# A four-layer graph stack on one core: row loads reordered, plane copies tied behind roundings, maps of h put ahead at a change of pair

## The chip, the cores and the metric

The kernel runs on one core of a Trainium2 chip. The metric is the device time of one execution in microseconds (us); the time of a version is the median of its runs. The engines have short names here: PE is the matrix engine (PEld its weight loads), DVE the vector engine, ACT the scalar engine, POOL the GpSimd engine and SP the sync engine, which here only issues DMAs. Each engine works through its own queue of instructions in order.

## The reference, cut to what matters

`x` is 8 batches of 2048 nodes with 64 features; `adj` is a 2048 x 2048 row-normalised adjacency matrix in float32. Four layers follow each other, each of them `x = x + layer(relu(layernorm(x)), adj)`:

```
layer 0:  A1 = A;  A2 = 2 A A - I;  out[n] = sum_k (A_k h)[n] @ w[n,k] + b[n]
          with w[n,k] = sum_d emb[n,d] W[d,k],  b[n] = emb[n] @ bias   (d = 16, k = 3)
layer 1:  v = h with node 0 set to a given vector; three times:
          v = relu([v, A v] @ W1.T + b1) @ W2.T + b2
layer 2:  (A h) * c, mixed by two small weights, then @ w_out.T + b_out
layer 3:  attention with mask adj > 0.5, softmax, then elu
```

The kernel uses that every row of `adj` has one value for all its non-zero entries and that no entry exceeds 0.5. It tests both on the way. If a test fails, a flag sends the program into a second, general path; with these inputs the flag stays 0. With no entry above 0.5 the mask of layer 3 is empty, its softmax is uniform, and its attention is the mean of h over all nodes.

## The kernel before, in words

**Tiling.** The 8 batches are four pairs p; a pair's two batches of 64 features fill 128 partitions. The 2048 nodes are 16 chunks m of 128 and four blocks nb of 512. `BT` holds the sign pattern (0 or 1) of the whole matrix in SBUF, 16 rows of chunks of 1 MiB. A product with the matrix is 16 chunks times two matmuls of 128 x 512: an operand is split into a rounded part H (`halves`, L274: an ACT copy to the fast matmul type) and the rest L (L282: a DVE subtraction that reads H), and both are multiplied with `BT` (L305). The factor of each row (`crow`) is applied when PSUM is read (`scaled`, L287, its DVE instruction L290).

**Loading (L380 to L660).** POOL issues the loads of the 16 rows (`load_adj`, L387), of the blocks of `x` (L155), of the four blocks on the diagonal `dg` (`load_dg`, L374; these give each row's value) and of the weights. `pool_loads` (L395) chains them in the order of a list. `plan[k]` is the list of what is issued after the k-th POOL power instruction (`powers`, L239, the 1/sqrt of the layer norm). ACT turns each row into signs in two halves (`sign`, L412). PE runs 8 matmuls of pair 0 and 6 of pair 1 as soon as a row is signed (`step`, L553). `bias_products` (L470) are two float32 matmuls with DVE copies to `bnb`. `make_cols` (L381) takes the diagonal on DVE, `make_crow` (L419) turns it by PE (`pt_c`) and DVE.

**Layer 0 (`node_weights`, L811).** For each of 4 blocks x 4 sub-blocks t, PE computes `y` (L825) in two groups of 12 matmuls from the three operands t0T, t1T, t2T, and DVE adds it into `acc` and `odd` with the embeddings (L834, 8 instructions each). `y` has two buffers in PSUM. After each t the function `between(nb, t)` (L877) runs side work: `join_planes` (t0T of the next block, ACT L195), `split_next`, which pops one `store_planes` (L172, two ACT copies into the single buffer `pl`, then a POOL DMA to DRAM, L173), and `halve_next`, which makes H and L of the next pair's operand (for pair 0 from PE transposes `pt_t`).

**Layers 1 and 2.** `step1` (L1013) is one of the three steps of layer 1 for a pair: sums of A v (`chunks`), maps by weights (`map_two`, `ph`, L1024), an addition and relu (`add`, L1057, L1058), and the maps of the result (`finish_two`, `back_two` L750, 64 small matmuls to `bn`). `finish_two` of blocks 2 and 3 is put off by `carry` into the next step or the next pair. At a change of pair, `halve_two` (again `back_two`, to `bn_u`) makes the new pair's last two operands from `gT`; it stands ahead of the carried `finish_two`. `layer2` works the same way with one product for each block. `go_on` (L253) advances the layer norms that are under way by a stage; `ahead` names a DVE instruction that they are put behind. At the end, `sums`, `keep_warm` (matmuls that nobody reads, L112) and `outputs` (L1194, L1199) finish layer 3.

**What sets the order.** The program is written as one sequence; a list scheduler with its own model of times turns it into the engines' queues, and may put a later instruction ahead of an earlier one on the same engine when it takes the earlier for not ready. `with tc.issue_after(ins):` adds an edge: the block's instructions on the engine of `ins` stand behind `ins` in that queue. It adds no semaphore.

```
plan = {
    1: ((row, 5), (xb, 4), (row, 6)), 2: ((xb, 5), (row, 7), (load_emb, 0)),
    3: ((row, 8),), 4: ((load_bias, 0), (row, 9), (xb, 6)),
    5: ((row, 10), (xb, 7), (row, 11), (row, 12)), 6: ((row, 13), (dia, 0), (row, 14)),
    7: ((row, 15), (dia, 1), (dia, 2), (dia, 3)) + tuple((load_wt, i) for i in range(K)),
}
```

Of the kernel before, what the change touches and what calls it, by code (L numbers as in the profile page):

```python
# [32 lines left out]
def kernel(tc: tile.TileContext, *args):  # L33
    nc = tc.nc
    with tc.tile_pool(name="flagp", bufs=1) as flagp:
        flag = flagp.tile([1, 1], I32, name="flag")
        uniform_path(tc, flag, *args)
        other = nc.values_load(flag[0:1, 0:1], min_val=0, max_val=1)
        with tc.If(other > 0):
            general_path(tc, *args)  # L40

# [2 lines left out]
def uniform_path(  # L44
# [132 lines left out]
    def split_next():  # L177
        if splits:
            splits.pop(0)()
# [381 lines left out]
    for _ in range(2):  # L561
        load_x01(nc.sync)
    row, dia, xb = load_adj, load_dg, lambda k: load_x01(nc.gpsimd)
    pool_loads(order[0], (
        (row, 0), (row, 1), (xb, 2), (row, 2), (xb, 3), (row, 3), (row, 4),
    ))
    with tc.issue_after(order[-1].ins):
        order.append(make_mask())
    for i in range(2):
# [12 lines left out]
    stage(1, 2)  # L582
    plan = {
        1: ((row, 5), (xb, 4), (row, 6)), 2: ((xb, 5), (row, 7), (load_emb, 0)),
        3: ((row, 8),), 4: ((load_bias, 0), (row, 9), (xb, 6)),
        5: ((row, 10), (xb, 7), (row, 11), (row, 12)), 6: ((row, 13), (dia, 0), (row, 14)),
        7: ((row, 15), (dia, 1), (dia, 2), (dia, 3)) + tuple((load_wt, i) for i in range(K)),
    }
    with tc.issue_after(order[-1].ins):
        pool_loads(powers[1], plan[1])  # L590
    for m in range(NCH):
        if m == 12:
            sign(14)
            sign(15)
            low()
            behind_v(lambda: turn_emb(last))
        if m % 2 and m < 12:
            k = m // 2 + 2
            norm_block(k)
            pool_loads(powers[k], plan[k])  # L600
            if k == 6:
                with tc.issue_after(order[-1].ins):
                    order.append(nc.gpsimd.tensor_tensor(
                        bd.rearrange("p (j c) -> p j c", c=C), bias8.to_broadcast([P, 8, C]),
                        mask.to_broadcast([P, 8, C]), op=ALU.mult,
                    ))
        if m == 13:
            behind_v(lambda: bias_products(last))

            def columns():  # L610
                for q in range(NB):
                    make_cols(q)
            behind_v(columns)
        last = step(0, m, banks[0])
        if m > 0:
            with tc.issue_after(last.ins):
                last = step(1, m - 1, banks[1])
        if m > 13:
            with tc.issue_after(last.ins):
                for nb in (0, 1) if m == 14 else (2, 3):  # L620
                    make_crow(nb)
# [112 lines left out]
        return lastp[0].tile([P, 512], F32, tag="fm", name=name, bufs=4)  # L734

    two = (slice(0, C), slice(C, P))

    def back_two(fTs, wmat, name):

        ps = psums[-1].tile([P, 2, 512], F32, tag="big", name=f"bn_{name}")
        for i, fT in enumerate(fTs):
            for t in range(4):
                for hf in range(2):
                    for bb in range(2):
                        at = t * P + hf * C
                        nc.tensor.matmul(  # L750
                            ps[two[hf], bb, (4 * i + t) * C:(4 * i + t + 1) * C],
                            fT[two[bb], at:at + C], wmat[two[bb], two[bb]],
                            start=True, stop=True,
                        )
        return ps.rearrange("p b (t c) -> p t b c", c=C)

    def back_whole(fT, wmat, name):
# [97 lines left out]
    for p in range(NP):  # L855
        hl_next, t1T_next = [], []

        loaded = {}

        def load_next(q):  # L860

            nm = f"0_{p + 1}_{q}"
            if p == 0:
                loaded[q] = l0q.tile([P, 512], F32, tag="hb", name=f"t1b_{nm}", bufs=3)
                nc.scalar.dma_start(loaded[q], t1D[:, q * 512:(q + 1) * 512])
            elif p + 1 < NP:
                loaded[q] = load_h(p + 1, q, nm, l0q)

        def halve_next(q):
            if q in loaded:  # L870
                src = loaded.pop(q)
                with tc.issue_after(chain[-1].ins):
                    hl_next.append(
                        back(src, 1, q) if p == 0 else halves(src, f"0_{p + 1}_{q}")
                    )

        def between(nb, t):  # L877

            if t == 2 and ahead_t0:
                join_planes(*ahead_t0)  # L880
            split_next()
            if t == 0 and 4 * p + nb + 1 < 4 * NP:
                at = divmod(4 * p + nb + 1, NB)
                ahead_t0.extend((load_planes(0, *at, l0q), term(0, "t0T_%d_%d" % at)))
            if t == 1 and p == 0:
                restage()
            if p + 1 == NP and t == 3 and nb > 1:
                begin_next(0, 3 * (nb - 2))
            if 4 * p + nb + 1 == 4 * NP:
                if t == 0:  # L890
                    begin_next(0, 2)
                if t < 3:
                    first_operand(t)
            elif nb == 2 and t == 1:
                halve_next(0)
            elif nb == 3:
                halve_next(t + 1)
                if t == 0:
                    load_next(3)

        def reload_t1(q):
            t = term(1, f"t1T_0_1_{q}")
            nc.sync.dma_start(t, t1D[:, q * 512:(q + 1) * 512])
            t1T_next.append(t)

        if p > 1:
            steps = make_weights()

            def behind(nb):
                if p + 1 < NP:  # L910
                    norm_0(p + 1, nb)
                elif nb in (0, 2):
                    next(steps)

            t1T, hl1 = term1(p, hl, behind)
        for nb in range(NB):
            nm = f"0_{p}_{nb}b"
            crow = load_crow(nb, nm)
            t2T = product(
                hl1, nb, nm, term(2, f"t2T_{nm}"), crow,  # L920
                fill={5: lambda: first_t0.append(
                    to_feat(h_first, term(0, "t0T_0_0"), "0_0_0")
                )} if p + nb == 0 else {},
                tag="mm" if p + nb else "b6",
            )
            if p + nb == 0:
                t0T = first_t0[0]
            go_on()
            ahead_t0 = []
            if p + nb == 0:  # L930
                pro.close()
                psums.append(ctx.enter_context(
                    tc.tile_pool(name="psum", bufs=2, space=bass.MemoryType.PSUM)
                ))
            if p == 0:
                restage()
            if nb == 3:
                load_next(2)
            if 4 * p + nb + 1 == 4 * NP:
                begin_next(0, 1)  # L940
            node_weights(p, nb, (t0T, t1T[nb], t2T), between)
            t0T = ahead_t0[-1] if ahead_t0 else None
            if nb in (1, 2):
                load_next(nb - 1)
            with tc.issue_after(kept[-1].ins):
                m = 4 * p + nb
                nc.gpsimd.dma_start(rows_of(MD, m), BTf[:, m, :])
            if p == 0:
                reload_t1(nb)
                norm_0(2, nb)  # L950
        if p == 0:
            hl1, t1T = hl_next, t1T_next
        else:
            hl = hl_next
# [58 lines left out]
    def step1(n, p, st, hl, gT):  # L1013
# [15 lines left out]
                for bb in range(2):  # L1029
                    nc.scalar.copy(gT[nb + i][two[bb], :], ph[bb][two[bb ^ i], :])  # L1030

        def finish_two(nb):
            ps = back_two(g_new[nb:nb + 2], w2T if last else w1e2, f"{nm}_{nb}")
            if not last:
                nc.vector.tensor_tensor(ps, ps, rows4(r1e, 8), op=ALU.add)
            for i in range(2):
# [32 lines left out]
        if st == 0:  # L1069
            fill = {4: lambda: begin_next(n, 3)} if n else {7: lambda: first_operand(3)}  # L1070
        chunks(ps0, hl, 0, halves_of[0], fill)
        if other:
            halve_two(n, 2)
        if carry:
            carry.pop()()
        map_two(0)
        ps1 = sums_of(1)
        chunks(ps1, hl, 1, halves_of[0])
# [12 lines left out]
        chunks(ps2, hl, 2, range(NCH), fill)  # L1091
        scale(ps2, 2)
        map_two(2)
        finish_two(0)
        add(2)
        go_on()
        fill = {}
# [9 lines left out]
        scale(ps3, 3)  # L1107
        add(3)
        go_on()
        carry.append(lambda: finish_two(2))  # L1110
        return hl_new, g_new

    def layer1(n, p):
# [19 lines left out]
    def finish2(g, count=1):  # L1133

        pn = back_two(es[g:g + count], wos, f"2_{g}")
        for i in range(count):
# [8 lines left out]
                acc, nm, lambda h: zs.update({k: h})  # L1145
            )
            later.append(norm) if i else norm()

    def sums(g):

# [13 lines left out]
        if nb == NB - 1 or g + 2 == NP * NB:  # L1164
            if not final:
# [11 lines left out]
                totals.append(total)  # L1177
                if g + 2 == NP * NB:
                    totals.pop()()
                    keep_warm("mm", 20)  # L1180
            else:
                for t in range(4):
                    nc.tensor.matmul(
# [4 lines left out]
    def outputs(p):  # L1188

        for nb in range(NB):  # L1190
# [5 lines left out]
                    op0=ALU.mult, op1=ALU.add  # L1196
                )
            queue = nc.scalar if nb % 2 == 0 and p == NP - 1 else nc.sync
            queue.dma_start(runs_of(out, p, nb), runs(acc))  # L1199

    def layer2(n, p):
        hl, _ = ops[n]
# [5 lines left out]

        def maps(g):
            if g == 0:  # L1210
                return carry.pop()()
            for k in (g - 4, g - 3):
                if k >= 0:
                    sums(k)
# [35 lines left out]
    for n, (layer, p) in enumerate(items):  # L1250
        (layer1, layer2)[layer - 1](n, p)
        if n == NP - 1:
            test_end()


@with_exitstack
# [590 lines left out]
```

## Time and profile before

| what | value |
|---|---|
| median of 3 runs | 1186.31 us (1185.85 to 1187.0) |
| the profiled execution's own time | 1184.05 us |
| its span, first to last instruction | 1182.3 us |
| PE busy | 1156.7 us, 98% of the span |
| DVE, ACT, POOL busy | 743.6, 293.6, 244.8 us |
| granted PE clock, mean | 0.995 |
| DMA | 147.02 MB, mean 124 GB/s |
| the chain that ended last | PE 78%, DVE 7%, DMA 5%, issue 4%, POOL 3%, ACT 2% |

The page has one column for each engine; busy is the union of its instructions. A wait stands in square brackets: how long the engine had been idle, and the instruction that ended it. In the timeline a row is start, duration, engine, line, operation, output and inputs. In the table by stretches each engine has its busy time and number of instructions, and PEclk is the share of the full clock that PE was granted. An idle PE is what this kernel can lose; on the other engines idle time costs nothing by itself.

### The profile page before, as it was taken

Reading aid. Unit: us, or ns where it says so; the run is one execution under the profiler, and the core shown is the slowest. Engines: PE = TensorE matmul, PEld = TensorE weight load, DVE = VectorE, ACT = ScalarE, POOL = GpSimd, SP = SyncE. Lnnn points to the kernel's source line nnn. Section 1 sums busy time; section 2 is a strip of 40 time slices with the busy share of each in tenths; the row PEclk is TensorE's granted clock in tenths of the full one; section 3 lists DMA queues with packets and bytes.
Section 4 is the critical chain, followed back from the end, with each engine's and each line's share of the span. In section 5 each row is a group of like instructions: output and inputs, shape, how many; then the busy total and the mean of one; then the engine's idle time right before and its main releaser. Section 6 shows DMA issues by size and latency. Waiting matters only on the chain.

```text
span 1182.3 us, 19454 instructions
## 1 busy us (share of the span) xinstructions
PE 1156.7 (98%) x7614; PEld 803.1 (68%) x7614; DVE 743.6 (63%) x1933; ACT 293.6 (25%) x465; POOL 244.8 (21%) x259
## 2 busy tenths in 40 slices
PE   9999999999999999999999999999999999999995
PEld 7775545555585555855557777777777777788884
DVE  5457878877847777267774437544653655466574
ACT  6621222111121111111113334334323433211110
POOL 5621322211132111101111004002300400241121
PEclk9999999999999999999999999999999999999998
DMA  9973555323352235312229534664863374451432
GB/s 355 354 211 91 152 147 129 103 67 76 76 160 68 67 82 99 93 32 68 64 61 210 127 89 130 161 137 102 171 134 94 122 169 101 118 177 53 136 117 66
DMA packets 131478, 147.02 MB, mean 124 GB/s; under 512 B 77512, under 2 KB 90312, under 8 KB 129328
## 3 DMA queue, kind: packets, MB, share of 16 engines
q1 hardware_dynamic: 114496, 86.25, 29.5%
q0 software_dynamic: 13456, 53.66, 15.1%
q10 hardware_dynamic: 3424, 5.77, 1.5%
q8 instruction: 62, 1.02, 0.3%
q14 instruction: 40, 0.33, 0.1%
HBM read 88.74 MB, written 39.59 MB: 109 GB/s over the span
## 4 chain that ended last, share of the span: by engine, by line
PE 78%; DVE 7%; DMA 5%; issue 4%; POOL 3%; ACT 2%; POOLq 0%; SPq 0%; DVEq 0%; ACTq 0%
PE bv L305 34%; PE y L825 25%; DMA BT<-in_adj_dram 3%; PE bv_3b L305 3%; PE bv_2b L305 3%; PE bv_1b L305 3%; PE bn L750 2%; PE ph L1024 2%; POOL rstd L239 1%; PE bv_0a L305 1%; PE bv_0b L305 1%; PE bv_2a L305 1%; PE bv_1a L305 1%; DVE acc L834 1%; DVE odd L834 1%
## 5 line engine op out<-in xcount | busy, mean ns | idle before, releaser
L305 PE MATMUL bv<-BT,H 128*128 128x512 f32 x768 | 302.8, 394 | 0.0
L305 PE MATMUL bv<-BT,L 128*128 128x512 f32 x768 | 299.3, 390 | 0.1
L834 DVE SCALAR_TENSOR_TENSOR acc<-y,emb,acc 128x128 f32<-128x128 f32 x512 | 176.3, 344 | 57.9 <-PE y L825 57.6
L305 PEld LDWEIGHTS bv<-BT,H 128*128 128x128 f32 x768 | 144.1, 188 | 37.2 <-PE bn L750 6.5
L305 PEld LDWEIGHTS bv<-BT,L 128*128 128x128 f32 x768 | 144.2, 188 | 29.7 <-DVE L L282 0.5
L834 DVE SCALAR_TENSOR_TENSOR odd<-y,emb,odd 128x128 f32<-128x128 f32 x448 | 153.4, 342 | 0.0
L239 POOL TENSOR_TENSOR rstd<-var,mhalf 128x8 f32<-128x8 f32 x64 | 106.4, 1663 | 184.8 <-DVE var L236 184.5
L825 PE MATMUL y<-wt,t0T 64*128 64x512 f32 x512 | 138.2, 608 | 4.7 <-DVE odd L834 3.9
L305 PE MATMUL bv<-BT,H_u 128*128 128x512 f32 x256 | 100.7, 393 | 0.4 <-DVE L_u L282 0.4
L305 PE MATMUL bv<-BT,L_u 128*128 128x512 f32 x256 | 100.0, 391 | 0.0
L290 DVE TENSOR_TENSOR g<-bv,crow 128x512 f32<-128x512 f32 x48 | 33.1, 689 | 96.0 <-PE bv L305 96.0
L231 ACT ACTIVATE sq<-z 128x512 f32<-128x512 f32 x64 | 40.4, 632 | 204.2 <-DVE z L226 130.0
L825 PEld LDWEIGHTS y<-wt,t0T 64*128 64x128 f32 x512 | 44.4, 186 | 68.4 <-issue 60.9
L806 POOL TENSOR_TENSOR acc<-acc,wl 128x512 f32<-128x512 f32 x16 | 22.7, 1419 | 307.0 <-DVE z L226 306.4
L806 POOL TENSOR_TENSOR acc<-acc,b2r 128x512 f32<-128x512 f32 x16 | 21.3, 1329 | 251.9 <-DVE z L226 251.9
L242 DVE SCALAR_TENSOR_TENSOR z<-z,rstd 128x512 f32<-128x512 f32 x64 | 43.6, 687 | 41.2 <-POOL rstd L239 41.2
L825 PE MATMUL y<-wt,t1T 64*128 64x512 f32 x256 | 67.7, 596 | 0.0
L172 ACT COPY pl<-z 128x512 uint16<-128x512 uint16 x48 | 27.3, 615 | 132.9 <-DVE z L242 99.9
L987 DVE SCALAR_TENSOR_TENSOR junk<-mt,cols,st 128x512 uint8<-128x512 bf16 x64 | 47.9, 748 | 16.6 <-DMA mt<-MD 15.9
L305 PEld LDWEIGHTS bv<-BT,H_u 128*128 128x128 f32 x256 | 48.0, 188 | 14.5 <-PE bn L750 2.4
L305 PEld LDWEIGHTS bv<-BT,L_u 128*128 128x128 f32 x256 | 48.1, 188 | 10.6 <-DVE L_u L282 0.8
L226 DVE SCALAR_TENSOR_TENSOR z<-mean,acc 128x256 f32<-128x256 f32 x112 | 52.4, 513 | 2.7 <-DMA hs<-z 1.2
(228 smaller groups left out, 1780.7 us busy)
## 6 DMA issues: line engine op xcount, KB each, us to landing
BT<-in_adj_dram POOLq DMA_DIRECT2D x16, 1024.0 KB, 10.4
crow<-crowD SPq DMA_DIRECT2D x64, 256.0 KB, 3.4
st<-in_adj_dram SPq DMA_DIRECT2D x64, 256.0 KB, 4.1
xs<-acc POOLq DMA_DIRECT2D x32, 256.0 KB, 2.7
MD<-BT POOLq DMA_DIRECT2D x16, 512.0 KB, 5.1
acc<-xs SPq DMA_DIRECT2D x32, 256.0 KB, 4.2
hp<-pl POOLq DMA_DIRECT2D x31, 256.0 KB, 2.8
acc<-in_x_dram SPq DMA_DIRECT2D x24, 256.0 KB, 4.6
```

The costliest lines, as they stand in the source:

```text
L172: nc.scalar.copy(pl[:, s], hv[:, s])
L226: firsts.append(nc.vector.scalar_tensor_tensor(split(z)[:, :, e], each(mean)[:, :, e, None].to_broadcast([P, 4, C]), -1.0 / C, nodes(xt)[: ...
L231: squares.append(nc.scalar.activation(sq, z, AF.Square))
L239: powers.append(nc.gpsimd.tensor_tensor(rstd, var, mhalf, op=ALU.pow))
L242: scales.append(nc.vector.scalar_tensor_tensor(groups(h), g, 0.0, rstd[:, :, None].to_broadcast([P, 8, C]), op0=ALU.max, op1=ALU.mult))
L290: ahead.append(nc.vector.tensor_tensor(to, ps.rearrange("p (q t) -> p t q", t=4), crow, op=ALU.mult))
L305: nc.tensor.matmul(ps, hl[m // 4][i][:, m % 4, :], BT[:, m, nb * 512:(nb + 1) * 512], start=(m == 0 and i == 0), stop=(m == NCH - 1 and i ...
L750: nc.tensor.matmul(ps[two[hf], bb, (4 * i + t) * C:(4 * i + t + 1) * C], fT[two[bb], at:at + C], wmat[two[bb], two[bb]], start=True, stop= ...
L806: nc.gpsimd.tensor_tensor(nodes(acc), nodes(acc), more, op=ALU.add)
L825: nc.tensor.matmul(y[:, bb, :], terms[k][hs_, ts], wt[hs_, k, dg * 512:(dg + 1) * 512], start=(k == 0), stop=(k == K - 1),)
L834: last = nc.vector.scalar_tensor_tensor(xj, yd, ec, old, op0=ALU.mult, op1=ALU.add)
L987: nc.vector.scalar_tensor_tensor(junk, mt, cols[:, i, :], st, op0=ALU.mult, op1=ALU.not_equal, accum_out=bad[:, i, q:q + 1],)
```

## The change

It has seven edits. (a) In the first list, row 3 stands ahead of block 3 of `x`. In `plan`, rows 9 to 15 move to an earlier entry where they can (row 9 from 4 to 3, 10 and 11 from 5 to 4, 13 from 6 to 5, 15 from 7 to 6), and the bias load and the diagonals 1 to 3 move with them: diagonal 1 now stands ahead of row 15. (b) The diagonals' DVE work is cut in two: columns 0 and 1 ahead of the bias products' copies, 2 and 3 behind them. (c) In `between`, `split_next` is put behind the last DVE addition of `y` and behind the last rounding copy written so far. (d) The carried `finish_two` is cut into its maps (PE) and its additions; at a change of pair the maps stand ahead of `halve_two`, the additions behind it. (e) After the last block's norm has begun, `go_on` puts the other norm's stages behind its first DVE instructions. (f) The warming matmuls near the end are put behind the last maps. (g) SP's read of the flag is put behind the last output DMA.

```diff
@@ tile_gnn_stack_kernel
+        last = uniform_path(tc, flag, *args)
+        with tc.issue_after(last.ins):
+            other = nc.values_load(flag[0:1, 0:1], min_val=0, max_val=1)
@@ loads
-        (row, 0), (row, 1), (xb, 2), (row, 2), (xb, 3), (row, 3), (row, 4),
+        (row, 0), (row, 1), (xb, 2), (row, 2), (row, 3), (xb, 3), (row, 4),
...
-        3: ((row, 8),), 4: ((load_bias, 0), (row, 9), (xb, 6)),
-        5: ((row, 10), (xb, 7), (row, 11), (row, 12)), 6: ((row, 13), (dia, 0), (row, 14)),
-        7: ((row, 15), (dia, 1), (dia, 2), (dia, 3)) + tuple((load_wt, i) for i in range(K)),
+        3: ((row, 8), (row, 9)), 4: ((xb, 6), (row, 10), (row, 11), (load_bias, 0)),
+        5: ((xb, 7), (row, 12), (row, 13)),
+        6: ((row, 14), (dia, 0), (dia, 1), (row, 15), (dia, 2), (dia, 3)),
+        7: tuple((load_wt, i) for i in range(K)),
@@ m == 13
+            def columns(qs):
+                for q in qs:
+                    make_cols(q)
+            behind_v(lambda: columns((0, 1)))
             behind_v(lambda: bias_products(last))
-            behind_v(columns)
+            behind_v(lambda: columns((2, 3)))
@@ between
-            split_next()
+            with tc.issue_after(chain[-1].ins), tc.issue_after(copies[-1].ins):
+                split_next()
@@ step1
-        def finish_two(nb):
-            ps = back_two(g_new[nb:nb + 2], w2T if last else w1e2, f"{nm}_{nb}")
+        def maps_two(nb):
+            return back_two(g_new[nb:nb + 2], w2T if last else w1e2, f"{nm}_{nb}")
+
+        def finish_two(nb, ps):
...
+        rest = carry.pop()() if carry else None
         if other:
             halve_two(n, 2)
-        if carry:
-            carry.pop()()
+        if rest:
+            rest()
...
-        carry.append(lambda: finish_two(2))
+        def put_off():
+            ps = maps_two(2)
+            return lambda: finish_two(2, ps)
+
+        carry.append(put_off)
@@ finish2
+            if g + i + 1 == NP * NB:
+                ahead.append(firsts[-1])
@@ sums
-                    keep_warm("mm", 20)
+                    with tc.issue_after(mapped[-1].ins):
+                        keep_warm("mm", 20)
```

In `back_two` each matmul is now kept in the list `mapped`, `outputs` keeps its DMAs in `written`, and `uniform_path` returns the last of them.

More of the change, by code (lines that the diff above doesn't have):

```diff
@@ L36 @@
         flag = flagp.tile([1, 1], I32, name="flag")
-        uniform_path(tc, flag, *args)
-        other = nc.values_load(flag[0:1, 0:1], min_val=0, max_val=1)
+        last = uniform_path(tc, flag, *args)
+        with tc.issue_after(last.ins):
+            other = nc.values_load(flag[0:1, 0:1], min_val=0, max_val=1)
         with tc.If(other > 0):
@@ L607, in uniform_path @@
         if m == 13:
+            def columns(qs):
+                for q in qs:
+                    make_cols(q)
+            behind_v(lambda: columns((0, 1)))
             behind_v(lambda: bias_products(last))
-            def columns():
-                for q in range(NB):
-                    make_cols(q)
-            behind_v(columns)
+            behind_v(lambda: columns((2, 3)))
         last = step(0, m, banks[0])
@@ L736, in uniform_path @@
     two = (slice(0, C), slice(C, P))
+    mapped = []
     def back_two(fTs, wmat, name):
@@ L749, in back_two @@
                         at = t * P + hf * C
-                        nc.tensor.matmul(
+                        mapped.append(nc.tensor.matmul(
                             ps[two[hf], bb, (4 * i + t) * C:(4 * i + t + 1) * C],
@@ L753, in back_two @@
                             start=True, stop=True,
-                        )
+                        ))
         return ps.rearrange("p b (t c) -> p t b c", c=C)
@@ L1093, in step1 @@
         map_two(2)
-        finish_two(0)
+        finish_two(0, maps_two(0))
         add(2)
@@ L1198, in outputs @@
             queue = nc.scalar if nb % 2 == 0 and p == NP - 1 else nc.sync
-            queue.dma_start(runs_of(out, p, nb), runs(acc))
+            written.append(queue.dma_start(runs_of(out, p, nb), runs(acc)))
+    written = []
     def layer2(n, p):
@@ L1210, in maps @@
             if g == 0:
-                return carry.pop()()
+                return carry.pop()()()
             for k in (g - 4, g - 3):
@@ L1253, in uniform_path @@
             test_end()
+    return written[-1]
 @with_exitstack
```

## The prediction

> **What bounds the kernel now.** I read the page first: PE is busy for 1156.7 of 1182.3 us, and the chain that ended last is 78% PE. The change takes no matmul away, so it can only win idle PE time, or time at a lower clock. Then the table by stretches, to see where PE idles:
>
> ```profile
> 11.00:40.00 29.00, 28.20 (x120) 21.39 (x119) 15.74 (x31) 21.24 (x27) 15.38 (x20) 1.00 1.03 379
> 40.00:56.00 16.00, 14.54 (x60) 10.58 (x60) 7.23 (x14) 10.04 (x14) 8.73 (x11) 1.00 1.04 375
> 166.00:171.00 5.00, 5.00 (x16) 2.53 (x18) 2.34 (x10) 0.90 (x2) 0.72 (x1) 0.66 0.15 52
> 620.00:1034.00 414.00, 410.14 (x3654) 322.47 (x3646) 218.99 (x395) 143.35 (x237) 63.19 (x65) 1.00 0.56 133
> 1160.00:1172.00 12.00, 8.59 (x110) 7.16 (x108) 5.94 (x13) 0.96 (x2) 3.27 (x2) 1.00 0.01 2
> ```
>
> First column of numbers behind the length: PE busy. PE loses 0.8 and 1.46 us while rows are loaded, 3.9 us in layer 1, 3.4 us at the end; from 166 to 171 it is busy at 0.66 of its clock, behind an idle 1.95 us (below). The change has a part for each of these places.
>
> **Splits behind roundings (edit c).** The timelines of ACT, DVE and PE at that place, in this order:
>
> ```profile
> 161.38 1.14 ACT L172 COPY pl<-z 128x512 uint16<-128x512 uint16 x2 [3.21 <-DMA hp<-pl]
> 162.43 0.57 ACT L280 CAST H_t<-pt_t 128x512 fp32r<-128x512 f32 x1
> ```
> ```profile
> 163.03 0.69 DVE L282 TENSOR_TENSOR L_t<-pt_t,H_t 128x512 fp32r<-128x512 f32 x1 [2.67 <-ACT H_t L280]
> ```
> ```profile
> 162.96 1.02 PE L825 MATMUL y<-wt,t2T_2b 64*128 64x512 f32 x4
> 165.94 1.29 PE L825 MATMUL y<-wt,t0T 64*128 64x512 f32 x4 [1.95 <-DVE odd L834]
> 166.95 1.98 PE L825 MATMUL y<-wt,t1T 64*128 64x512 f32 x4
> 168.66 1.82 PE L825 MATMUL y<-wt,t2T_2b 64*128 64x512 f32 x4
> ```
>
> The transposes pt_t start on PE at 157.98 and end about 158.6. Their rounding H_t could run then, but a plane copy stands ahead of it on ACT and waits for the DMA out of the single buffer pl. DVE waits for H_t, additions queue behind, both buffers of y stay full, PE stops. In the program that copy comes one sub-block later than the rounding; the queue has them swapped. The tie undoes the swap: H_t at 158.7, L_t at 160.36 (where DVE went idle), the next additions at 161.4 with their y, and 8 of them (0.26 us apart) end at 163.5; PE wants that buffer at 163.82. So the next group starts at 163.82, not 165.94: 2.12 us. Then the clock: four matmuls take 0.86 us from start to start at 161.25 and 1.71 from 166.95 and 1.62 from 168.66; the group of 12 takes 4.34 us (165.94 to 170.28) instead of 2.67: 1.67 us. [...] The row shows 0.66 right behind it; I take the row: 3.8 instead of 2.1 us. The copy itself loses nothing: its DMA ends at 161.3 either way. In block 3, roundings at 186.53 to 198.41 stand among the copies with no PE wait, so 0 there; the cover is 0.84 us of DVE wait that PE did not feel. The tie to DVE touches no DVE instruction (a split is two ACT copies and a POOL DMA): 0. What the tie adds: copies, and the join t0T behind them on ACT, now wait for a rounding that waits for PE. Bounds -0.2 and 3.9 us.
>
> **Maps ahead at a change of pair (d).** PE, the same at 824.66 and 928.58:
>
> ```profile
> 720.88 0.69 PE L750 MATMUL bn_u<-w1e,gT 64*64 64x64 f32 x32
> 722.42 0.69 PE L750 MATMUL bn_u<-w1e,gT 64*64 64x64 f32 x32 [0.85 <-ACT gT L195]
> 722.93 1.11 PE L750 MATMUL bn<-wl,g 64*64 64x64 f32 x64
> ```
>
> 32 maps take 0.51 us from start to start, so PE loses 1.03 us before 722.42, at 825 as much, at 929 0.83. The 64 maps bn move into that hole. They need the relu of block 3 for their second half; it ends at 721.09, and PE gets there at 721.39. Order: bn to 721.91, first bn_u to 722.42, second as before. The rounding H_u stays at 723.18, ph moves up by the whole hole; its next operand L_u ends at 725.8, the chunks reach it at 727.5. Both PSUM buffers are held as before, and the additions stand behind L_u as before. Sum 1.03 + 1.03 + 0.83 = 2.9 us (bounds 1.5, if the relu comes late, and 3.0).
>
> **End (e, f, g).** DVE, then PE:
>
> ```profile
> 1163.54 0.69 DVE L242 SCALAR_TENSOR_TENSOR z<-z,rstd 128x512 f32<-128x512 f32 x1 [1.81 <-POOL rstd L239]
> 1164.15 0.68 DVE L1143 TENSOR_TENSOR acc<-bn,acc 128x512 f32<-128x512 f32 x1
> ```
> ```profile
> 1161.23 0.94 PE L112 MATMUL warm<-ones 128*128 128x128 f32 x6
> 1162.10 0.69 PE L750 MATMUL bn<-wl,e 64*64 64x64 f32 x32
> ```
>
> The last operand e is ready at 1161.65; warming matmuls hold bn to 1162.10 (0.4 us), and DVE waits for another block's POOL result while acc could run at 1162.8. Now acc starts at 1162.45 instead of 1164.15 (1.70), and the copy four (0.2) leaves the chain; the other block's z moves behind and runs while ACT squares. The chain then goes on with the same durations: about 1.8, of which I take 1.7, since four or z may land in its way. SP's read of the flag moves from 1034.6 (0.67 us) behind the last output DMA, issued at 1175.0. All engines wait there until 1179.3 for the DMAs; the read hides in those 4.3 us; without cover it would cost about 1.0. At 1034 it frees SP for loads that nobody on PE waits for: 0. Bounds 1.0 and 2.0.
>
> **Loads (a, b).** POOL's timeline, PE's weight loads, the stretches:
>
> ```profile
> 38.41 0.59 POOL L387 DMA_DIRECT2D BT<-in_adj_dram  x1
> ```
> ```profile
> 45.05 0.19 PEld L553 LDWEIGHTS bv_0a<-BT,H 128*128 128x128 f32 x1 [0.88 <-ACT BT L412]
> ```
> ```profile
> 36.00:38.00 2.00, 2.00 (x10) 1.61 (x9) 0.60 (x2) 1.67 (x2) 1.22 (x1) 1.00 1.02 391
> 38.00:40.00 2.00, 2.00 (x10) 1.67 (x9) 0.96 (x2) 0.98 (x2) 2.00 (x4) 1.00 0.64 147
> 64.00:66.00 2.00, 2.00 (x13) 1.64 (x12) 2.00 (x18) 0.13 (x1) 0.55 (x1) 1.00 1.08 154
> ```
>
> Row 10 is issued at 38.41, when the queue has run dry: 147 GB/s for 2 us against 391, a hole of about 1.3 us. Issued with plan 4 (31.5) it closes. PE's waits for rows 3, 10 and 11, with the slow restart behind each, sum to 0.76 + 1.21 + 1.36 = 3.3 us (starts less 0.23 a matmul). That is the ceiling; but PE needs 14 x 0.232 = 3.25 us a row and the rows come at about that pace, so what is won is about the hole. Row by row: signs of 10 and 11 start at 42.6 and 46.5 (43.94, 48.53), of 15 at 62.2; PE, 0.76 ahead from row 3, still waits 0.7, 0.65 and 0.5 at rows 10, 11 and 13, and reaches row 15 at 64.05 instead of 65.59: 1.5 us. Against it stands diagonal 1, now ahead of row 15. Its runs are 512 B. [...] 0.26 MB would take 0.67 us at 391 GB/s. The row of 64 to 66, where diagonals load, says 154 GB/s: 1.7 us. With 0.67 row 15 would be signed from 61.2, with 1.7 from 62.2; I took the second. POOL issues six loads instead of three in plan 6 (about 4.2 us from 44.7, then bd 1.1), ready at 50.0 for a power due at 50.2: 0, and 0.5 if that cover goes. Columns 0 and 1 (8 x 0.21 us on DVE) now hold back the copies bnb until diagonal 1 lands (about 58.5), and PE's second bias product behind them: up to 1 us, I take 0, as PE is at row 14 until 59. Row 3 ahead of x block 3 delays a norm by 1.3 us that ACT reaches later. Bounds 0 and 2.8.
>
> **Sum.** 3.75 + 2.9 + 1.7 + 1.5 = 9.85 us: the span goes to 1172.5, the profiled execution from 1184.05 to 1174.2. The median of the runs stands 2.3 us above that execution, so I subtract from it: 1186.31 - 9.85 = 1176.5.
>
> **Rivals.** *The stall moves*: with L_t early, DVE has both norm stages (1.2 us) and L_t (0.6) to catch up, and PE waits for y anyway. Then 3.75 is missing: 1180.2. Against it: 8 additions end 0.3 us before PE's need; that is little. *The loads give nothing*: diagonals ahead of row 15, bnb behind diagonal 1: PE waits once late for what it gained: 1178.0. *Slower*: the tie makes new stalls of the old kind. ACT already waits up to 2.1 us for a rounding H whose buffer PE's products bv_3b must free; a copy, and the join, now stand behind such roundings at t = 1 to 3 of block 3 in three pairs. A stall of this kind costs 3.85 with its clock; four give 1186.3 - 9.85 + 15.4 = 1191.9, and three are where it turns slower. Against it: no copy waits near those roundings now (the next is at 305.4, the rounding at 291.6). *The change does nothing*: the edges only confirm what the scheduler had; 1186.3. But the queue shows the swap.
>
> **How the numbers follow.** Likeliest case 0.67 at 1176.5 (its own range 1174 to 1178), loads nothing 0.15, stall moves 0.12, nothing 0.03, slower 0.03. The range 1173.5 to 1180.5 takes in the first three, and at its low end the upper bounds of all parts (3.9 + 3.0 + 2.0 + 2.8 = 11.7, so 1174.6) and 1 us of spread. Within 0.2% (2.4 us, what a measurement of this kernel can tell from no change) only the fourth: faster 0.94, same 0.03, slower 0.03.
>
> **What would show it.** H_t ahead of the waiting pl copy, no clock below 1.00 between 40 and 1170; bn ahead of bn_u at three places with no PE wait; acc of the last block ahead of the other z, last additions about 1.7 us earlier after the last product; no DMA hole at 38 to 40, row 15 near 64. It is wrong if PE stops at a new place, above all in blocks 2 and 3 of layer 0, or if PE waits near 58 to 66 for diagonals.

## The result, and the profile after

The median of 7 runs after is 1178.81 us (1175.3 to 1181.25); beside them the kernel before had 1186.03 us. The ratio is 0.994, with a 95% interval of 0.9921 to 0.996: 7.1 us less (4.7 to 9.4), where 9.85 were forecast. The profiled execution took 1180.88 us, with a span of 1179.2 us; it is one of the longer ones of its kernel. Timelines and tables below have the columns of those shown of before.

The table by stretches, of after:

```profile
11.00:40.00 29.00, 27.93 (x115) 20.34 (x114) 15.35 (x30) 20.76 (x25) 15.28 (x18) 1.00 1.07 410
40.00:56.00 16.00, 16.00 (x72) 13.01 (x71) 9.39 (x20) 13.24 (x17) 12.43 (x15) 1.00 1.07 403
158.00:171.00 13.00, 13.00 (x61) 7.16 (x58) 11.14 (x38) 3.67 (x6) 1.46 (x2) 1.00 0.48 140
614.00:1028.00 414.00, 409.91 (x3583) 320.59 (x3582) 218.10 (x390) 142.97 (x236) 60.57 (x63) 1.00 0.55 131
```
From 40 to 56 us PE no longer waits for rows (16.00 of 16 us, from 14.54); from 11 to 40 it waits a little more than before (27.93 of 29, from 28.20). The stall and the low clock in block 2 of layer 0 are gone (13.00 of 13 us at clock 1.00). Layer 1 did not get better: PE is busy for 409.91 of 414 us there, from 410.14.

**Block 2 of layer 0**: ACT, DVE and PE of after.

```profile
156.58 0.58 ACT L281 CAST H_t<-pt_t 128x512 fp32r<-128x512 f32 x1 [0.52 <-PE pt_t L317]
159.24 1.14 ACT L173 COPY pl<-z 128x512 uint16<-128x512 uint16 x2 [2.07 <-DMA hp<-pl]
```
```profile
158.19 0.68 DVE L283 TENSOR_TENSOR L_t<-pt_t,H_t 128x512 fp32r<-128x512 f32 x1
```
```profile
160.87 1.02 PE L828 MATMUL y<-wt,t2T_2b 64*128 64x512 f32 x4
161.73 1.07 PE L828 MATMUL y<-wt,t0T 64*128 64x512 f32 x4
```
The rounding H_t stands ahead of the plane copies, which wait for their DMA alone. DVE meets its L_t without a wait, and PE goes on where it had stood for 1.95 us.

**The first change of pair**: PE, DVE, and the chain that ended last (start, length, what), of after.

```profile
715.43 1.16 PE L753 MATMUL bn<-wl,g 64*64 64x64 f32 x64
716.41 1.24 PE L753 MATMUL bn_u<-w1e,gT 64*64 64x64 f32 x64
717.48 1.04 PE L1028 MATMUL ph<-gT,wl 64*64 64x512 f32 x8
...
722.25 0.39 PE L306 MATMUL bv<-BT,H_u 128*128 128x512 f32 x1
724.92 0.50 PE L306 MATMUL bv<-BT,L_u 128*128 128x512 f32 x1 [2.28 <-DVE L_u L283]
```
```profile
716.66 0.69 DVE L1046 TENSOR_TENSOR acc<-bn,acc 128x512 f32<-128x512 f32 x1 [1.01 <-PE bn L753]
722.06 0.69 DVE L1046 TENSOR_TENSOR acc<-bn,acc 128x512 f32<-128x512 f32 x1 [4.71 <-DMA acc<-xs]
...
724.18 0.68 DVE L283 TENSOR_TENSOR L_u<-bn_u,H_u 128x512 fp32r<-128x512 f32 x1
```
```profile
711.20 1.64 POOL rstd L240
712.84 4.86 DMA xs<-acc
...
717.76 4.20 DMA acc<-xs
...
722.06 0.69 DVE acc L1046
722.75 0.66 DVE mean L225 x2
...
724.26 0.61 DVE L_u L283
```
The maps bn do fill the hole: no bracket on the three rows of maps. But 5 us later PE stops for 2.28 us at the first product with L_u. The operand of this L_u was there long before (its H_u ran on ACT from 717.72 to 718.30). DVE stood at the second put-off addition, which waits for its block of `x`: that block was stored to DRAM at 712.84, and its reload landed at 721.96. Behind the wait, the second addition, both means and one z (722.06 to 724.18) still ran ahead of L_u. In the kernel before, the queue of DVE had both L_u ahead of both additions, and the additions had no wait:

```profile
723.80 0.69 DVE L282 TENSOR_TENSOR L_u<-bn_u,H_u 128x512 fp32r<-128x512 f32 x1 [2.66 <-ACT H_u L280]
725.14 0.69 DVE L282 TENSOR_TENSOR L_u<-bn_u,H_u 128x512 fp32r<-128x512 f32 x1 [0.65 <-ACT H_u L280]
725.75 1.28 DVE L1040 TENSOR_TENSOR acc<-bn,acc 128x512 f32<-128x512 f32 x2
```

**The end**: DVE and PE of after, then DVE of before.

```profile
1159.71 0.68 DVE L291 TENSOR_TENSOR e<-bv,crow 128x512 f32<-128x512 f32 x1
...
1161.21 0.69 DVE L1154 TENSOR_TENSOR acc<-bn,acc 128x512 f32<-128x512 f32 x1 [0.74 <-PE bn L753]
...
1163.34 0.69 DVE L243 SCALAR_TENSOR_TENSOR z<-z,rstd 128x512 f32<-128x512 f32 x1
...
1168.90 0.42 DVE L1208 SCALAR_TENSOR_TENSOR acc<-pS,acc 128x256 f32<-128x256 f32 x1 [1.25 <-PE pS L1197]
```
```profile
1160.45 0.69 PE L753 MATMUL bn<-wl,e 64*64 64x64 f32 x32 [0.39 <-DVE e L291]
1161.08 3.17 PE L113 MATMUL warm<-ones 128*128 128x128 f32 x26
```
```profile
1160.97 0.68 DVE L290 TENSOR_TENSOR e<-bv,crow 128x512 f32<-128x512 f32 x1
...
1171.86 2.74 DVE L1194 SCALAR_TENSOR_TENSOR acc<-pS,acc 128x256 f32<-128x256 f32 x8 [1.25 <-PE pS L1183]
```
The maps bn start before the warming matmuls, and the addition stands ahead of the other block's z. From the start of e to that of the last additions are 9.19 us (1159.71 to 1168.90), from 10.89 (1160.97 to 1171.86).

**Loads**: the stretch of after, and the first matmul of PE on row 15 for pair 0, before and after.

```profile
38.00:40.00 2.00, 2.00 (x11) 1.63 (x10) 0.43 (x1) 1.12 (x2) 2.00 (x2) 1.00 1.07 415
```
```profile
65.59 0.48 PE L553 MATMUL bv_0a<-BT,H 128*128 128x512 f32 x1
```
```profile
63.51 0.48 PE L554 MATMUL bv_0a<-BT,H 128*128 128x512 f32 x1
```
The hole of the transfers at 38 to 40 us (147 GB/s) is closed (415 GB/s), and PE reaches row 15 2.1 us earlier.

### The profile page after: what moved, and what is told of

Same layout as the page of the kernel before. It is cut to its first block, busy times and chain, and to the rows that moved or that the text cites. A ratio compares the mean times of both kernels' runs of the same rounds, so it can differ in the third digit from the quotient of the medians.

```text
span 1179.2 us, 19459 instructions
## 1 busy us (share of the span) xinstructions
PE 1157.1 (98%) x7614; PEld 802.6 (68%) x7614; DVE 745.2 (63%) x1933; ACT 293.9 (25%) x465; POOL 243.6 (21%) x259
## 4 chain that ended last, share of the span: by engine, by line
PE 79%; DVE 7%; DMA 6%; issue 4%; POOL 2%; ACT 1%; POOLq 0%; ACTq 0%; DVEq 0%; SPq 0%
PE bv L306 32%; PE y L828 26%; PE bv_2b L306 3%; PE bv_1b L306 3%; PE bv_3b L306 3%; PE bv_0b L306 2%; PE bn L753 2%; PE ph L1028 2%; DMA acc<-xs 2%; DVE z L227 2%; DMA xs<-acc 2%; POOL rstd L240 1%; DMA BT<-in_adj_dram 1%; PE bv_2a L554 1%; PE bv_1a L554 1%
## 5 line engine op out<-in xcount | busy, mean ns | idle before, releaser
L232 ACT ACTIVATE sq<-z 128x512 f32<-128x512 f32 x64 | 40.4, 632 | 202.3 <-DVE z L227 126.3
L227 DVE SCALAR_TENSOR_TENSOR z<-mean,acc 128x256 f32<-128x256 f32 x112 | 54.8, 532 | 2.6 <-ACT pl L173 2.1
L1034 ACT COPY g<-ph 64x512 f32<-64x512 f32 x64 | 37.2, 581 | 68.9 <-PE ph L1028 67.8
```

The lines of the kernel that those rows point to most:

```text
L227: firsts.append(nc.vector.scalar_tensor_tensor(split(z)[:, :, e], each(mean)[:, :, e, None].to_broadcast([P, 4, C]), -1.0 / C, nodes(xt)[: ...
L232: squares.append(nc.scalar.activation(sq, z, AF.Square))
```

## The experiments

In the expectations, theory A says that the put-off additions stand in DVE's queue ahead of L_u and hold it back until their reload of `x` has landed; B and C are the rivals, told with their numbers there.

**1. Additions behind L_u** (after, with this edit; called kernel 1 below)

```diff
         if rest:
-            rest()
+            with tc.issue_after(lows[-1].ins):
+                rest()
```


> The changed kernel with one more tie: the carried additions (and the norm they begin) stand behind the last L_u subtraction on DVE. Theory A (the order of the additions on DVE makes the new stall at a change of pair: the second addition waits for its block of x, L_u stands behind it, PE waits for L_u): no PE wait over 0.3 us behind the ph maps at the three changes of pair, no clock below 1.00 there, about 5 us under the changed kernel's median: 1173 to 1175, and the runs close together. Theory B (the late block of x holds DVE in any order, and PE waits for the next thing that DVE makes, the scaled sums): the stall only moves by some us; the time stays at 1178 to 1179. Theory C (the new PE wait is a late rounding H_u on ACT, not DVE): no change, 1178 to 1179.

Measured: 1174.04 us (1172.92 to 1175.92), ratio 0.9916 (0.9899 to 0.9932). As A said: from 700 to 945 us no wait of PE is over 0.3 us. It is faster than the kernel before; its interval still overlaps that of the kernel after, and experiments 9 to 11 compare the two again. The clock and PE in the 8 us behind the first change of pair, first of after, then of this kernel (the changes lie within 1 us of each other):

```profile
723.00:731.00 8.00, 6.08 (x19) 4.59 (x20) 5.20 (x10) 2.85 (x5) 3.84 (x4) 0.79 0.25 76
```
```profile
723.00:731.00 8.00, 8.00 (x37) 6.63 (x36) 8.00 (x14) 1.99 (x3) 4.91 (x6) 1.00 0.36 125
```
19 matmuls against 37, by the idle time and by a clock of 0.79.

**2. Maps back** (after, without edit d)

```diff
-        rest = carry.pop()() if carry else None
         if other:
             halve_two(n, 2)
-        if rest:
-            rest()
+        if carry:
+            carry.pop()()()
```


> The changed kernel with edit (d) alone undone: maps and additions both behind the operands of the new pair, as before. Theory A: the three waits of about 1 us for gT come back, the stall goes: the sum of the other parts alone, 2.1 (loads) + 3.9 (ties) + 1.0 to 1.7 (end) = 7.0 to 7.7 under before, so 1178.5 to 1179, near the changed kernel's median but with a narrow spread. Theory B or C (the stall is not made by edit (d)): the waits come back and the stall stays: 1181 to 1184.

Measured: 1177.51 us (1176.62 to 1178.64), ratio 0.9942 (0.9926 to 0.9958). That is 1 us below what A gave, and far from B and C. The three waits for gT are back (0.82 to 0.85 us) and the stall is gone. So all the other edits together give what the kernel after gives (0.994): edit d as made adds nothing.

**3. Ties of the splits alone** (before, with edit c)

```diff
-            split_next()
+            with tc.issue_after(chain[-1].ins), tc.issue_after(copies[-1].ins):
+                split_next()
```


> The kernel before with edit (c) alone, the splits behind the last rounding. My theory: the stall at 163 and the half clock behind it go, 3.8 us: 1182.2, PEclk 1.00 throughout, and no new wait in layer 0. Rival (the stall goes only because the loads shifted the DMA times): PE still waits about 2 us there and the time is within 1 us of before.

Measured: 1181.37 us (1179.29 to 1185.47, 22 runs), ratio 0.9975 (0.9966 to 0.9984): 3.0 us (1.9 to 4.0).

**4. Maps ahead alone** (before, with edit d; cut as in the diff of the change)

```diff
+        rest = carry.pop()() if carry else None
         if other:
             halve_two(n, 2)
-        if carry:
-            carry.pop()()
+        if rest:
+            rest()
```


> The kernel before with edit (d) alone. Theory A: it wins 0.9 us three times and loses 4 us or less at each change of pair, where L_u stands behind the additions on DVE: no gain in sum, 1184 to 1189, with a wider spread than before. Theory B (edit (d) is harmless, the stall comes from the other edits' shift of the DMA times): 1183.1, with no PE wait for L_u.

Measured: 1185.2 us (1179.56 to 1190.54, 22 runs), ratio 1.0005 (0.9993 to 1.0017). Here too the maps give nothing, and the runs spread over 11 us, those of the kernel before beside them over 6.3.

**5. Loads alone** (before, with edits a and b: the lists of the diff and the columns in two parts)

```diff
-        3: ((row, 8),), 4: ((load_bias, 0), (row, 9), (xb, 6)),
+        3: ((row, 8), (row, 9)), 4: ((xb, 6), (row, 10), (row, 11), (load_bias, 0)),
...
-            behind_v(columns)
+            behind_v(lambda: columns((2, 3)))
```


> The kernel before with the loading order and the diagonal's columns of the change alone. Theory: the profiles so far give the start of the first y after loading: 89.85, 91.82 and 91.87 us in three kernels that load as before (mean 91.18), 87.75, 86.55 and 87.80 us in three that load as after (mean 87.37). So loading is worth 3.8 us and not the 1.5 us of the prediction nor the 2.1 us of the first pair of traces: a ratio to the kernel before near 0.997, and the hole of the transfers at 38 to 40 us closed. Rival 1, the prediction's term: 1.5 us, a ratio of 0.9987. Rival 2: the gain is spent again in the stall in block 2 of layer 0, ratio 1.000.

Measured: 1182.07 us (1178.62 to 1185.27), ratio 0.9984 (0.997 to 0.9997): 1.9 us (0.4 to 3.6). The hole is closed (432 GB/s from 38 to 40). The interval holds the prediction's 1.5 us, and the theory's 3.8 us lies just outside. Rival 2 (ratio 1.000) lies just outside too, so a part of the gain may still be lost in block 2.

**6. The end alone** (before, with edits e and f)

```diff
+            if g + i + 1 == NP * NB:
+                ahead.append(firsts[-1])
...
-                    keep_warm("mm", 20)
+                    with tc.issue_after(mapped[-1].ins):
+                        keep_warm("mm", 20)
```


> The kernel before with the two ties of the end alone (the last block's step behind the first chains, the filler matmuls behind the maps). Theory: the 1.70 us of the stretch from the last e to the last sum that the traces of before and after show are kept whole, since nothing else runs there: a ratio of 0.9986, and the wait ahead of the last pS of 1.9 us falls to about 1.3 us, that ahead of the first pS behind bn from 1.7 us to under 0.7 us. Rival: the gain belongs to the order that the other edits leave behind and not to these ties: ratio 1.000.

Measured: 1182.35 us (1178.52 to 1187.03), ratio 0.9983 (0.9969 to 0.9998): 2.0 us (0.2 to 3.7). In its timeline of PE the maps at the end follow e by a wait of 0.40 us, and the wait ahead of the last pS is 1.12 us (1.74 in before):

```profile
1166.04 0.69 PE L751 MATMUL bn<-wl,e 64*64 64x64 f32 x32 [0.40 <-DVE e L290]
...
1173.30 1.16 PE L1187 MATMUL pS<-z,ones 128*128 128x128 f32 x8 [1.12 <-DVE z L242]
```

**7. The flag's read as before** (kernel 1, that of experiment 1, without edit g)

```diff
-        last = uniform_path(tc, flag, *args)
-        with tc.issue_after(last.ins):
-            other = nc.values_load(flag[0:1, 0:1], min_val=0, max_val=1)
+        uniform_path(tc, flag, *args)
+        other = nc.values_load(flag[0:1, 0:1], min_val=0, max_val=1)
```


> The kernel after with the additions behind both L_u (as in the earlier run of that) and the flag's load and read as in the kernel before. Theory: the tie of the flag is worth nothing, since the two waits of TensorE in the first products of layer 2 (1039 and 1055 us there, 0.60 and 0.73 us) stand in kernels with the flag as before as well (0.84 and 0.71 us where the splits alone were tied): same ratio as with the additions behind, 0.9916 within 0.1%. Rival: the tie of the flag makes those waits, and without it 1.3 us more are gained, a ratio near 0.9905.

Measured: 1174.53 us (1174.11 to 1174.82), ratio 0.9927 (0.991 to 0.9944). The intervals of 0.9916 and 0.9927 overlap, so no cost and no gain of the read is shown; the rival's 0.9905 is not met.

**8. Without the ties** (after, without edit c: the diff of 3 turned round)

> The kernel after without the tie of the splits behind the roundings. Theory: the stall in block 2 of layer 0 comes back, 2.5 to 3.9 us of it, whatever the loading order: a ratio to the kernel before about 0.003 above that of the kernel after (0.994), so near 0.997, and the run from the first y of block 2 to the next at 20.5 to 21.9 us against 18.0 us. Rival: with the new loading order the splits fall elsewhere and the tie changes nothing, ratio 0.994 and 18 us.

Measured: 1181.1 us (1178.43 to 1185.53), ratio 0.9982 (0.9968 to 0.9995), 0.0042 above the kernel after: 5.0 us, more than the 2.5 to 3.9 expected, but the 0.997 lies within the interval. PE has its stall again, with all the rest of the change in place:

```profile
162.52 1.13 PE L828 MATMUL y<-wt,t0T 64*128 64x512 f32 x4 [1.98 <-DVE odd L837]
163.45 1.86 PE L828 MATMUL y<-wt,t1T 64*128 64x512 f32 x4
```

**9 to 11. Only the second addition behind L_u**, and beside it, on one chip, kernel 1 once more and the kernel after once more. The edit of 9, on the kernel after:

```diff
-                    nc.vector.tensor_tensor(nodes(acc), pn, nodes(acc), op=ALU.add)
+                    behind = tc.issue_after(lows[-1].ins) if i and other_pair else nullcontext()
+                    with behind:
+                        nc.vector.tensor_tensor(nodes(acc), pn, nodes(acc), op=ALU.add)
...
-            rest()
+            rest(bool(other))
```


> The kernel after with only the second of the two put-off additions behind both L_u at a change of pair; the first, with its mean and its z, stays ahead of them in DVE's queue. Theory (the wait for the reload of x is the cost): the first addition's block lands early (714.16 us, the second's at 721.96 in the kernel after), so what is left ahead of L_u is DVE work of 0.7 + 0.7 + 0.8 us that fits into DVE's idle time there: the three changes of pair within 0.5 us of the kernel with both additions behind (107.8 to 108.3 us in sum, from the last maps of block 3 to those of block 0 of the next pair, against 111 to 115 us), and the run within 1 us of it. Rival (the additions' own DVE work ahead of L_u is the cost, so half of it stays): the three changes at about 110 to 111 us and the run 2 to 2.5 us above it.

> The kernel after with both additions behind both L_u once more, beside the one above and the kernel after on the same chip: 4 to 5 us below the kernel after (1174.04 against 1178.81 us so far), with a spread of 3 us or less against its 6.

> The kernel after itself, beside the two above. If the wait for the reload is what spreads its time (1175.3 to 1181.25 us), the three changes of pair sum to 111 to 115 us in its profile again and no other stretch differs from the kernel with both additions behind by more than 1 us, but for loading, which has varied by 3 us among kernels that load alike. Ratio to the kernel before 0.994 within 0.002. Rival: the first profile of the kernel after was an outlier and the changes sum to 110.5 us as before.

Measured, in this order: 1174.35 us (1172.98 to 1175.28), ratio 0.9905 (0.989 to 0.992); 1176.0 us (1174.25 to 1177.16), ratio 0.9916 (0.9903 to 0.9929); 1180.02 us (1176.22 to 1182.02), ratio 0.9945 (0.9927 to 0.9963). DVE of the first of them:

```profile
716.11 0.69 DVE L1048 TENSOR_TENSOR acc<-bn,acc 128x512 f32<-128x512 f32 x1 [0.97 <-PE bn L753]
716.84 0.69 DVE L225 TENSOR_REDUCE mean<-acc 128x8 f32<-128x512 f32 x1
717.56 0.76 DVE L227 SCALAR_TENSOR_TENSOR z<-mean,acc 128x256 f32<-128x256 f32 x2
719.55 0.69 DVE L283 TENSOR_TENSOR L_u<-bn_u,H_u 128x512 fp32r<-128x512 f32 x1 [1.23 <-ACT H_u L281]
721.23 0.69 DVE L283 TENSOR_TENSOR L_u<-bn_u,H_u 128x512 fp32r<-128x512 f32 x1 [0.99 <-ACT H_u L281]
721.84 0.68 DVE L1048 TENSOR_TENSOR acc<-bn,acc 128x512 f32<-128x512 f32 x1
```
The first addition still stands ahead of L_u, with its mean and z, and costs nothing; the second finds its block landed. So the first addition's work is not the cost. What costs is the second addition's wait for its reload, with the work that queues up behind that wait (2.1 us in the kernel after). The kernel after, profiled again, stalls at the same place (its second addition waits 4.64 us, PE 2.22 us). The intervals of 9 and 11 do not overlap; those of 10 and 11 just touch. Two expectations were missed in part. 9 is 1.65 us below 10, not within 1 us of it; and 10 is longer than 11 by 1.2 and 1.9 us in the two stretches between the changes, for reasons that are open. With the second or both additions behind L_u the runs spread over 2.3 to 3 us, against 6.

## Why the prediction came near in the total and was wrong in a step

This table is worked out from the traces, one execution of each kernel. "First y": where loading and the first products have ended. "Block 2": from the y behind the transposes pt_t to the y behind the next products (156.48 to 174.51 us in after). "Changes": the sum of the three changes of pair, each from the last group of ph of one pair to the second group of the next (for after the first is 700.7 to 741.1). "End": from the first pS to the end of the span.

| profiled kernel | first y | block 2 | changes | end |
|---|---|---|---|---|
| before | 89.85 | 21.92 | 110.57 | 117.62 |
| 3, c alone | 91.82 | 18.03 | 109.56 | 118.16 |
| 4, d alone | 91.87 | 20.55 | 111.17 | 118.88 |
| 5, a and b alone | 89.22 | 22.61 | 110.55 | 117.54 |
| 6, e and f alone | 93.08 | 22.41 | 110.53 | 116.33 |
| after | 87.75 | 18.03 | 114.94 | 116.40 |
| 11, after again | 89.38 | 18.03 | 113.91 | 116.72 |
| 8, after without c | 86.40 | 21.93 | 111.64 | 116.52 |
| 2, after without d | 87.80 | 18.03 | 111.03 | 116.83 |
| 1, both behind L_u | 86.55 | 18.05 | 107.79 | 116.34 |
| 10, 1 again | 87.50 | 18.05 | 108.25 | 116.74 |
| 7, 1 without g | 88.88 | 18.05 | 108.29 | 116.28 |
| 9, second behind L_u | 87.33 | 18.03 | 108.23 | 117.08 |

**Splits (c), 3.75 us: right.** Block 2 takes 18.0 us in all eight kernels with the tie and 21.9 us on average (20.55 to 22.61) in the five without: 3.85 us. The runs gave 3.0 us (experiment 3) and 5.0 us (8). The 20.55 is experiment 4, where the clock stayed at 1.00 behind a wait of 2.30 us; so the clock's part of the term, 1.67 us, does not come with every such wait (last section). The rival "the stall moves" would have shown a wait in the same column, and "slower" new stalls in later blocks. From the end of this column to block 3 of the next pair every kernel takes 116.64 to 116.71 us, and to the last y of layer 0 the kernels with the tie take 434.7 us on average, those without 434.8. Neither came.

**Maps (d), 2.9 us: wrong, and the one step that failed.** The prediction moved ph up by the whole hole. That happened: against before, after is 5.48 us ahead at 701 and 6.39 us at the ph of the change, 0.91 of the 1.03 us. Then it said that "the additions stand behind L_u as before". They did not: at all three changes both additions stand ahead of both L_u in DVE's queue in the four kernels with d as made, and behind both in the five with the old maps; no edge held them. Why the scheduler did so is not shown, but it fits that bn now ends at 716.59 us, before H_u (718.30), where in the kernel before it ended at 724.04, behind the start of L_u (723.80). The second addition waits for a store and a load through DRAM (4.86 and 4.20 us at the first change of after), and with it waits L_u. The mean of the five kernels with the old maps is 110.45 us; the four with d as made take 112.9 on average (111.17 to 114.94), so 2.5 us worse; the four with d and an addition behind L_u take 108.14, so 2.3 us better. The runs show less of a loss: d alone costs 0.6 us (from a gain of 0.8 to a loss of 2.0), and with and without d the change gives 0.994. The size 2.9 was near the truth for a change with that edge. By the prediction's own signs the step was wrong: PE stops at a new place (2.28 us), and the clock is below 1.00 behind it (0.79 from 723 to 731 us); but it looked for that place in layer 0.

**End (e, f), 1.7 us: right.** 1.70 us from e to the last additions in the first pair of traces, 1.5 us in the column (116.6 on average against 118.05), 2.0 us (0.2 to 3.7) in the runs. **Flag (g), 0: not contradicted** by experiment 7.

**Loads (a, b), 1.5 us: the mechanism right, the size open.** In the first pair of traces PE reaches row 15 at 63.51 us, where 64.05 was forecast, and its waits of 0.7, 0.65 and 0.5 us at rows 10, 11 and 13 did not come. The nine kernels with the new order reach the first y at 87.9 us on average (86.40 to 89.38), the four with the old one at 91.7 (89.85 to 93.08): 3.8 us; the run alone gave 1.9 us. Kernels that load alike differ by 3 us, and experiment 5's own trace is only 0.6 us ahead of that of before, so the size stays open between them. One term was measured: the prediction gave the diagonal of 0.26 MB ahead of row 15 a time of 1.7 us, from the 154 GB/s of a stretch in which diagonals load, and put aside its other estimate, 0.67 us, from the 391 GB/s measured while rows load. In the trace of after diagonal 1 lands 0.83 us behind diagonal 0 (55.75 and 56.58), among rows: the smaller estimate was nearer. Row 15 lands at 59.7 us, from 62.1. Edits a and b, like e and f, were only run together.

**The sum.** Worked out of the columns: 3.85 - 2.5 + 1.5 + 3.8 = 6.6 us. By the runs of one part each (experiments 3 to 6): 3.0 - 0.6 + 2.0 + 1.9 = 6.3 us. Both stand beside 7.1 measured. Either way d is the large error: it was forecast 5.4 us too high by the columns, 3.5 by the runs; the loads were 2.3 or 0.4 us too low. That the total came near is in part luck: 1178.81 lies above the likeliest case's 1174 to 1178, and within the range up to 1180.5, which was that wide for two rivals, neither of which came. (Two of its sums are slightly off: 2.12 + 1.67 is 3.79 where 3.75 was taken, and 1.70 + 0.2 is 1.9 where "about 1.8" stands.) With one edge more, the kernel of experiment 1 or 9 has what the prediction was about: its 0.9916 and 0.9905 of about 1185 us are 10 to 11 us less.

## What to carry to other kernels

When a list scheduler fills the queues, moving an instruction earlier also makes its consumers ready earlier, and they may pass the very operand that the move was to bring forward, as the additions passed L_u here: after each move, look at the queue order of every engine that reads the result, and tie what can wait. Look above all for a consumer with a second operand that comes through memory: what stands behind it in its queue waits with it, as L_u did here behind an addition that waited 4.71 us. And when edits of both signs are put in together, a total near the forecast does not show that the steps were right; each was settled only by a run of its own.

## What the runs showed of the hardware that was not expected

A wait of PE of about 2 us did or did not bring its clock down, and its length did not decide. Around waits of 1.95 us (before), 1.98 us (experiment 8), 2.28 us (after), 2.66 us (5) and 2.73 us (6) the granted clock was 0.66, 0.66, 0.79, 0.72 and 0.72 in stretches of 5 to 8 us; behind 2.30 us (4) and 2.22 us (11) it was 1.00. In before and after the clock behind the wait is low in one stretch of 3.41 us, at 0.50. The stretch begins 0.84 us behind the end of the wait in before and 1.07 us in after (725.99 us); in before:

```profile
166.78:170.19 3.41, 3.41 (x10) 1.63 (x8) 1.08 (x5) 0.12 (x1) 0.72 (x1) 0.50 0.22 77
```
What set the waits that brought the clock down apart from the others is not shown. Behind the one of 1.95 us the next 12 matmuls of y took 4.34 us (165.94 to 170.28), where 12 of after, at a clock of 1.00, took 2.59 us (161.73 to 164.32): it cost about 1.7 us more than itself.

In the trace of after, the store `xs<-acc` of 256 KB took 4.86 us from issue to landing for the second block at the first change of pair (4.76 us in 11), but 2.4 us for the first block there and 2.4 to 3.1 us for the blocks at the second and third change. Why it is longer there was not tried; with the reload of 4.20 us behind it, the first change is the longest of the three in after (40.4, 37.5 and 37.0 us).
